# Cross-attention in a decoder layer: the scores of both token halves in one run of matmuls, the value products of both halves in another

## The chip, the cores and the metric

The kernel runs on one core of a Trainium2 chip. The metric is device time in microseconds of one execution, from the first to the last instruction with what lies around them. Names used below: PE is TensorE (matrix products), PEld its weight loads, DVE is VectorE, ACT ScalarE, POOL GpSimd, SP the engine whose queue issues most transfers.

## The reference

One decoder layer over 32 sequences of 64 tokens, width 512, everything in fp32: block-sparse self-attention, cross-attention to a second sequence, and a feed-forward part, each followed by a residual sum and a layer norm. Only the cross-attention is touched here:

```
q = (x @ Wq + bq).reshape(B, L, 8, 4, 128)            # 32 query heads, 8 key heads
k, v = split(ctx @ Wkv + bkv)                          # 8 key heads of 128
scores = einsum('blkgd,bmkd->bkglm', q, k) / sqrt(128) # 64 x 64 for each sequence and head
o = einsum('bkglm,bmkd->blkgd', softmax(scores), v)
x = layernorm(x + o.reshape(B, L, 4096) @ Wo + bo)
```

## The kernel before

The cross-attention stage works on 32 units `n`: eight key heads `g` (outer) by four blocks `tb` of 512 tokens (inner). One block holds eight sequences of 64 tokens; its two halves `pr` = 0 and 1 are 256 tokens each. A unit needs queries for four heads (`qx`), scores (`sx`), a softmax, transposed probabilities (`pTx`), value products (`pox`) and a projection back to width 512 (`wx`).

The query and output projections are each done as seven products of halved matrices instead of eight (a Strassen-like scheme). A product is one `step(i)` of class `Queries` or `Projection`: `mul` (the matmuls at L282) issues 4 matmuls of 128x128 weights with 256 columns, in the trace 8 passes, into one of three banks x, y, z; `read` then lets DVE (or ACT) add the bank into its destination. Two steps that use the same bank follow the same rule in both kernels: the later one waits until the earlier one has been read. For a projection the reads are L345 (one 128x512 sum) and, in step 1, L353 as well (128x1024). The left operands of steps 3, 5, 6 and 7 of a projection are sums that POOL makes from the attention output (`output_sums`, L256 to L259).

`scores(n, pr)` puts 16 small matmuls (128 rows by 64 columns, 64 columns moving, in the trace 32 passes) into a bank, then DVE and ACT do the softmax of this half: row maxima `mxx` (L1048), subtraction `ex` (L1050), exponential on ACT (L1051), sums `denx` (L1053), reciprocal (L1054), product (L1055, both inputs in SBUF), block transposition `Tx` (L1060). `move(n)` issues eight transfers on SP that give `pTx`. `attend(n, pr)` is four matmuls with 64 weight rows, two of them on the lower and two on the upper half of the array (8 passes), into two banks `po0` and `po1`; ACT and DVE empty these with two activations and two additions of the bias each (L1108, L1110).

PE and POOL follow the order written out in the loop over `n`; DVE's and ACT's order comes from the scheduler. While unit `n` makes queries and scores, unit `n-1` is attended and projected. The order on PE for an inner `n`, `q` for query steps and `w` for projection steps:

```
q1 q6 q5 q7 q2  attend(n-1,0)  q4  attend(n-1,1)  q3  w1  scores(n,0)  w6 w5  scores(n,1)  w7 w2 w4 w3
```

In every second unit POOL has four more operations here: for `tb` = 1 the sums of the next token block, for `tb` = 3 those of the next query weights. In the units of the first head (`g` = 0) it adds the output bias to the running sum, four operations of the same size.

PSUM has eight banks in this stage: four shared ones (tag `ps`), two for scores, one each for `po0` and `po1`.

Of the kernel before, what the change touches and what calls it, by code (L numbers as in the profile page):

```python
# [9 lines left out]
F32 = mybir.dt.float32  # L10
I32 = mybir.dt.int32
AF = mybir.ActivationFunctionType
ALU = mybir.AluOpType
# [3 lines left out]
P = 128  # L17
DIM = 512
NH, NKV, HD = 32, 8, 128
REP = NH // NKV  # L20
NT = 2048
SEQ = 64
# [30 lines left out]
def decoder_layer(  # L53
# [30 lines left out]
    nc = tc.nc  # L84
# [91 lines left out]
    HF = DIM // 2  # L176
# [71 lines left out]
    def output_tiles(name):  # L248
        return [big.tile([P, 2, TB], F32, tag=f"oT{j}", name=f"{name}_{j}") for j in range(2)]
# [214 lines left out]
    with ExitStack() as ph:  # L464
# [143 lines left out]
        def scores(n, i):  # L608


            g, tb, h = units[n]
            u = f"{g}_{tb}_{h}_{i}"
            s = sc.tile([P, 2, 512], F32, tag="sc", name=f"s{u}")
            for a in range(2):
                nc.tensor.matmul(  # L615
                    s[:, a, :HALF], qTs[n // REP][:, units[n][2], i * P : (i + 1) * P],
                    kTs[g][:, a * HALF : (a + 1) * HALF], start=True, stop=True,
                )
            nmax = small.tile([P, 1], F32, tag="nmax", name=f"nmax{u}")
            nc.vector.tensor_reduce(nmax, s[:, :, :HALF], AX.XY, ALU.max, negate=True)  # L620
            p = sb.tile([P, NKEY], F32, tag="p", name=f"p{u}", bufs=4)
            den = small.tile([P, 1], F32, tag="den", name=f"den{u}")
            nc.scalar.activation(  # L623
                p.rearrange("q (a k) -> q a k", a=2), s[:, :, :HALF], AF.Exp,
                bias=nmax, accum_out=den,
            )
            if i == 0:
                Ts[n] = sb.tile([P, NBK, TPB, SQ], F32, tag="T", name=f"T{g}_{tb}_{h}")
                flush()
            else:  # L630
                turn(n, i - 1)
            nc.vector.reciprocal(den, den)  # L632
            nc.vector.tensor_scalar(p, p, den, None, ALU.mult)  # L633
            ps_[n, i] = p
            if i == TPB - 1:
                turn(n, i)
# [301 lines left out]
    with ExitStack() as ph:  # L938
# [74 lines left out]

        NPR = TPB // 2
        units = [(g, tb) for g in range(NKV) for tb in range(NTB)]
        kvs, qTs, Ts, pTs, oTs, pjs = {}, {}, {}, {}, {}, {}

        def load_kv(n):
            g, tb = units[n]
# [10 lines left out]
            q = Queries(wq_cur[g], right.pop(n), qTs[n], f"q{u}", XYZ, bias)  # L1030
            return q

        def scores(n, pr):
            g, tb = units[n]
            u = f"x{g}_{tb}_{pr}"
            s = sc.tile([P, 2 * REP, SEQ], F32, tag="sc", name=f"s{u}")
            for i in range(2):
                for h in range(REP):
                    for b in range(2):
                        c0 = (2 * pr + i) * P + b * SEQ  # L1040
                        nc.tensor.matmul(  # L1041
                            s[b * SEQ : (b + 1) * SEQ, i * REP + h, :],
                            qTs[n][:, h, c0 : c0 + SEQ], kvs[n][:, pr, 0, c0 - pr * HF : c0 - pr * HF + SEQ],
                            start=True, stop=True,
                        )
            shape = [P, 2 * REP, SEQ]
            mx = small.tile([P, 2 * REP], F32, tag="mx", name=f"mx{u}")
            nc.vector.tensor_reduce(mx, s, AX.X, ALU.max)  # L1048
            e = sb.tile(shape, F32, tag="e", name=f"e{u}")
            nc.vector.tensor_tensor(e, s, mx[:, :, None].to_broadcast(shape), ALU.subtract)  # L1050
            nc.scalar.activation(e, e, AF.Exp, scale=SCALE)  # L1051
            den = small.tile([P, 2 * REP], F32, tag="xden", name=f"den{u}")
            nc.vector.tensor_reduce(den, e, AX.X, ALU.add)  # L1053
            nc.vector.reciprocal(den, den)  # L1054
            nc.vector.tensor_tensor(e, e, den[:, :, None].to_broadcast(shape), ALU.mult)  # L1055


            if pr == 0:
                Ts[n] = sb.tile([P, 2, TPB * REP, SQ], F32, tag="T", name=f"Tx{g}_{tb}", bufs=1)
            nc.vector.transpose(  # L1060
                Ts[n][:, :, pr * 2 * REP : (pr + 1) * 2 * REP, :].rearrange("p k r j -> p r k j"),
                e.rearrange("p r (k i) -> p r k i", i=SQ),
            )
# [13 lines left out]
                        )  # L1077
            pTs[n] = pT

        def attend(n, pr):  # L1080
            g, tb = units[n]
            if pr == 0:
                oTs[n] = output_tiles(f"oTx{g}_{tb}")
            o5 = [o.rearrange("d h (t b q) -> d t b h q", t=TPB, b=2) for o in oTs[n]]
            po = [
                pp.tile([P, 2, REP * SEQ], F32, tag=f"po{b}", name=f"pox{g}_{tb}_{pr}_{b}")
                for b in range(2)
            ]
            for i in range(2):
                for b in range(2):  # L1090
                    r = slice(b * SEQ, (b + 1) * SEQ)
                    t = 2 * pr + i
                    nc.tensor.matmul(  # L1093
                        po[b][:, i, :].rearrange("d (h a j) -> d h a j", h=REP, a=2),
                        kvs[n][r, pr, 1, i * HD : (i + 1) * HD],
                        pTs[n][r, :, t * P : (t + 1) * P].rearrange("p a (h j) -> p h a j", h=REP),
                        start=True, stop=True,
                    )

            bias = bv[:, g : g + 1]  # L1100
            for b in range(2):
                for j in range(2):
                    dst = o5[j][:, 2 * pr : 2 * pr + 2, b, :, :]
                    src = po[b][:, :, j * HF // 2 : (j + 1) * HF // 2].rearrange(
                        "d i (h q) -> d i h q", h=2
                    )
                    if b == 0:
                        nc.scalar.activation(dst, src, AF.Identity, bias=bias)  # L1108
                    else:
                        nc.vector.tensor_scalar(dst, src, bias, None, ALU.add)  # L1110
            if pr == 1:
                left = output_sums(oTs.pop(n), f"sox{g}_{tb}")
                pjs[n] = Projection(left, wo_cur[g], tb, f"wx{g}_{tb}", XYZ)
                del pTs[n], kvs[n]

        def project(n, *steps):
            g, tb = units[n]
            for i in steps:
                pjs[n].step(i)
                pjs[n].read()  # L1120
            if steps[-1] == 3:
                del pjs[n]
                if g == NKV - 1:
                    layernorm(tb, "x")
                    later.append(lambda: transpose_block(tb, "x2"))
# [84 lines left out]
        for n in range(N + 1):  # L1210
            if n < N:
                g, tb = units[n]
                q = queries(n)
                for i in (1, 6, 5, 7):
                    q.step(i)
                    q.read()
                q.corner()
                q.step(2)


                behind = g > 0 and tb == 1
                if not behind:
                    next_tokens(n + 1, 0)
            if n > 0:
                attend(n - 1, 0)
            while later:
                later.pop(0)()
            if n < N:
                q.step(4)
                q.read()  # L1230
            if n > 0:
                attend(n - 1, 1)
            if n < N:
                q.step(3)
                q.read()
                if behind:
                    next_tokens(n + 1, 0)
                next_tokens(n + 1, 1)
            if n == N:
                feed_forward(1)  # L1240
            if n > 0:
                project(n - 1, 1)
            if n < N:
                if n + 1 < N:
                    load_kv(n + 1)
                scores(n, 0)
            if n < N and g == 0:
                for j in range(TPB):
                    a = acc[tb][:, j, :]
                    nc.gpsimd.tensor_tensor(a, a, bo, ALU.add)  # L1250
            if n > 0:
                project(n - 1, 6, 5)
            if n < N:
                scores(n, 1)
                move(n)
                if tb == NTB - 1 and g + 1 < NKV:
                    load_xq(g + 1)
            if n > 0:
                project(n - 1, 7, 2, 4, 3)
                if n < N and tb == 0:  # L1260
                    if g > 0:
                        load_xo(g)
                    if g == NKV - 1:
                        load_ffn()
            if n == N - 1:
                feed_forward(0)
# [53 lines left out]
```

## Time and profile before

| what | us |
| --- | --- |
| median of 3 runs (3109.12 to 3114.3) | 3110.07 |
| the profiled execution, its own time | 3110.94 |
| its span, first to last instruction | 3109.0 |
| first scores of unit 0, of unit 1, of unit 31 | 2068.86, 2091.02, 2977.11 |
| from one unit's first scores to the next unit's, inner units | 29.26 after even n, 29.45 after odd n |
| PE, DVE, POOL busy over the whole span | 3059.1, 2199.3, 971.6 |

The stage starts at 2068.86 and its last value products are at 3016; the self-attention before it and the feed-forward part after it are the same in both kernels. Since a unit is repeated 32 times, a tenth of a microsecond in a unit is about 3 us in the total.

### The profile page before, as it was taken

The numbers are of one execution on the slowest core, as the hardware profiler recorded it, in microseconds if no ns is written. First come the engines' busy times: TensorE is split into PE (matmuls) and PEld (weight loads), VectorE is DVE, ScalarE is ACT, GpSimd is POOL, SyncE is SP. The second block draws the span as 40 slices with busy tenths as digits, with TensorE's granted clock in tenths as the row PEclk, the third lists the DMA queues.
The fourth block names the chain that finished last, engine by engine and source line by source line (L and its number), as shares of the span: only waits on it lengthen the run. The fifth ranks groups of instructions, "written<-read, shape, count | busy, mean of one in ns | idle before, by whom it ended". The sixth has DMA issues, their size and how long they took to land.

```text
span 3109.0 us, 42300 instructions
## 1 busy us (share of the span) xinstructions
PE 3059.1 (98%) x14944; PEld 2312.8 (74%) x14944; DVE 2199.3 (71%) x3957; ACT 757.3 (24%) x1760; POOL 971.6 (31%) x789
## 2 busy tenths in 40 slices
PE   8999999999999999999999999999999999999998
PEld 5677677777777777677777669988888888888864
DVE  6777777877877877877877754346666666656777
ACT  2323222222232232222322312211111111111222
POOL 3231321321322322223213122135454444444421
PEclk9999999999999999999999999999999999999999
DMA  6444444444454444444444453221121121121101
GB/s 203 118 112 119 113 115 123 111 123 112 107 130 111 107 123 118 105 126 115 114 110 110 100 140 121 101 94 48 53 64 48 51 66 48 48 69 48 48 28 41
DMA packets 200913, 298.66 MB, mean 96 GB/s; under 512 B 44160, under 2 KB 94848, under 8 KB 200704
## 3 DMA queue, kind: packets, MB, share of 16 engines
q1 hardware_dynamic: 187328, 282.51, 33.7%
q10 hardware_dynamic: 11328, 9.26, 1.0%
q0 software_dynamic: 2048, 4.20, 0.5%
q8 instruction: 120, 1.97, 0.3%
q14 instruction: 89, 0.73, 0.1%
HBM read 107.05 MB, written 20.97 MB: 41 GB/s over the span
## 4 chain that ended last, share of the span: by engine, by line
PE 91%; DVE 4%; DMA 2%; SPq 2%; ACT 1%; issue 1%; ACTq 0%; DVEq 0%
PE po L661 15%; PE s L615 15%; PE sx L1041 2%; PE pox L1093 2%; PE wx_0y L282 1%; PE wx_2y L282 1%; PE wx_1y L282 1%; SPq L653 1%; PE w_0y L282 1%; PE q_3y L282 1%; PE w_3y L282 1%; PE qx_0y L282 1%; PE qx_3y L282 1%; PE wx_3y L282 1%; PE q_2y L282 1%; PE w_1y L282 1%
## 5 line engine op out<-in xcount | busy, mean ns | idle before, releaser
L623 ACT ACTIVATE p<-s,nmax 128x576 f32<-128x576 f32 x512 | 379.2, 741 | 1213.6 <-DVE nmax L620 1210.6
L615 PE MATMUL s<-kT,qT 128*128 128x288 f32 x2048 | 578.0, 408 | 11.6 <-ACT p L623 10.8
L661 PE MATMUL po<-pT,v 128*128 128x512 f32 (+1 forms) x1280 | 549.3, 602 | 4.6 <-DMA pT<-T 4.6
L615 PEld LDWEIGHTS s<-kT,qT 128*128 128x128 f32 x2048 | 387.5, 190 | 116.5 <-issue 20.1
L620 DVE TENSOR_REDUCE nmax<-s 128x1 f32<-128x576 f32 x512 | 383.8, 750 | 48.9 <-PE s L615 48.3
L641 DVE STREAM_TRANSPOSE T<-p 128x576 f32<-128x576 f32 x512 | 393.8, 769 | 4.4
L661 PEld LDWEIGHTS po<-pT,v 128*128 128x128 f32 (+1 forms) x1280 | 213.6, 189 | 205.0 <-issue 177.6
L633 DVE TENSOR_SCALAR p<-p,den 128x576 f32<-128x576 f32 x512 | 324.9, 635 | 17.9
L632 DVE RECIPROCAL den<-den 128x1 f32<-128x1 f32 x512 | 83.9, 164 | 238.3 <-ACT p L623 238.3
L256 POOL TENSOR_TENSOR so<-oT,oT 128x512 f32<-128x512 f32 x32 | 42.6, 1330 | 651.1 <-ACT oT L684 651.1
L258 POOL TENSOR_TENSOR so<-oT 128x512 f32<-128x512 f32 x32 | 40.7, 1272 | 334.0 <-PE w_1y L282 93.0
L1051 ACT ACTIVATE ex<-ex 128x512 f32<-128x512 f32 x64 | 40.4, 631 | 328.1 <-DVE ex L1050 328.1
L1197 POOL TENSOR_TENSOR txx<-x1T 128x512 f32<-128x512 f32 x31 | 39.4, 1269 | 237.1 <-PE qx_3z L282 95.7
L197 POOL TENSOR_TENSOR tx<-xT 128x512 f32<-128x512 f32 x31 | 39.7, 1280 | 206.9 <-PE q_3z L282 65.5
L623 ACT ACTIVATION_READ_ACCUMULATOR p<-s,nmax 128x1 f32 x512 | 99.0, 193 | 0.0
L1110 DVE TENSOR_SCALAR oTx<-pox,bv 128x256 f32<-128x256 f32 x128 | 56.1, 478 | 47.8 <-PE pox L1093 47.8
L256 POOL TENSOR_TENSOR sox<-oTx,oTx 128x512 f32<-128x512 f32 x32 | 40.5, 1266 | 151.2 <-DVE oTx L1110 146.2
L684 ACT COPY oT<-po 128x512 f32<-128x512 f32 x128 | 71.8, 586 | 45.0 <-PE po L661 44.1
L1041 PEld LDWEIGHTS sx<-kvx,qTx 128*64 128x64 f32 x2048 | 64.8, 138 | 20.9 <-issue 11.3
L1093 PE MATMUL pox<-pTx,kvx 64*128 64x256 f32 x512 | 73.3, 402 | 1.4 <-DMA pTx<-Tx 1.4
L1041 PE MATMUL sx<-kvx,qTx 128*64 128x64 f32 x2048 | 73.5, 225 | 0.0
L1108 ACT ACTIVATE oTx<-pox,bv 128x256 f32<-128x256 f32 x128 | 53.7, 470 | 79.0 <-PE pox L1093 79.0
(445 smaller groups left out, 5786.5 us busy)
## 6 DMA issues: line engine op xcount, KB each, us to landing
pT<-T SPq DMA_DIRECT2D x1020, 80.0 KB, 2.1
pT<-T SPq DMA_DIRECT2D x1016, 64.0 KB, 2.0
xT<-in_xT SPq DMA_DIRECT2D x31, 1024.0 KB, 5.7
kvx<-kv SPq DMA_DIRECT2D x32, 512.0 KB, 3.3
pTx<-Tx SPq DMA_DIRECT2D x256, 64.0 KB, 2.0
kv<-c SPq DMA_DIRECT2D x30, 512.0 KB, 2.6
wo<-in_woT SPq DMA_DIRECT2D x32, 256.0 KB, 3.0
xwq<-in_xwq SPq DMA_DIRECT2D x32, 256.0 KB, 2.8
```

Of the source, the lines that this page charges most:

```text
L256: nc.gpsimd.tensor_tensor(t[1], a[1, 0], a[1, 1], ALU.add)
L282: nc.tensor.matmul(self.banks[b][:, m, :], self.left[i][:, k, m * P : (m + 1) * P], self.right[i][:, k, :], start=(first and m + k == 0), ...
L615: nc.tensor.matmul(s[:, a, :HALF], qTs[n // REP][:, units[n][2], i * P : (i + 1) * P], kTs[g][:, a * HALF : (a + 1) * HALF], start=True, s ...
L620: nc.vector.tensor_reduce(nmax, s[:, :, :HALF], AX.XY, ALU.max, negate=True)
L623: nc.scalar.activation(p.rearrange("q (a k) -> q a k", a=2), s[:, :, :HALF], AF.Exp, bias=nmax, accum_out=den,)
L632: nc.vector.reciprocal(den, den)
L633: nc.vector.tensor_scalar(p, p, den, None, ALU.mult)
L641: nc.vector.transpose(Ts[n][:, :, i, :], ps_.pop((n, i)).rearrange("q (b k) -> q b k", k=SQ))
L661: nc.tensor.matmul(pos[n].rearrange("d (a q) -> d a q", a=NQD), vs[units[n][0]][rows, v, :], pTs[n // 2][rows, :, chunk, :], skip_group_ch ...
L684: nc.scalar.copy(o[:, i, :].rearrange("d (t a k) -> d a t k", t=TPB, a=NQD), pos.pop(n - 1 + i).rearrange("d (a t k) -> d a t k", a=NQD, t ...
L1041: nc.tensor.matmul(s[b * SEQ : (b + 1) * SEQ, i * REP + h, :], qTs[n][:, h, c0 : c0 + SEQ], kvs[n][:, pr, 0, c0 - pr * HF : c0 - pr * HF + ...
L1093: nc.tensor.matmul(po[b][:, i, :].rearrange("d (h a j) -> d h a j", h=REP, a=2), kvs[n][r, pr, 1, i * HD : (i + 1) * HD], pTs[n][r, :, t * ...
```

## The change

`scores(n)` now issues the 32 small matmuls of both halves together and keeps both banks; the softmax of each half is a function of its own. `attend(n)` issues the value products of both halves together: the first half still goes to `po0` and `po1`, the second half to two of the four shared banks, and the emptying follows in the order half, head pair, batch. The loop places the joined `attend` behind query step 4, and the projection steps after the scores come as 6, 5, 2, 7, 3, 4:

```
q1 q6 q5 q7 q2  q4  attend(n-1)  q3  w1  scores(n)  w6 w5  w2 w7 w3 w4
```

```diff
-        def scores(n, pr):
+        def scores(n):
+            for pr in range(2):
+                g, tb = units[n]
+                s = sc.tile([P, 2 * REP, SEQ], F32, tag="sc", name=f"sx{g}_{tb}_{pr}")
+                for i in range(2):
+                    for h in range(REP):
+                        for b in range(2):
+                            c0 = i * P + b * SEQ
+                            nc.tensor.matmul(
+                                s[b * SEQ : (b + 1) * SEQ, i * REP + h, :],
+                                qTs[n][:, h, pr * HF + c0 : pr * HF + c0 + SEQ],
+                                kvs[n][:, pr, 0, c0 : c0 + SEQ], start=True, stop=True,
+                            )
+                ss[n, pr] = s
+
+        def softmax(n, pr):
             g, tb = units[n]
             u = f"x{g}_{tb}_{pr}"
-            s = sc.tile([P, 2 * REP, SEQ], F32, tag="sc", name=f"s{u}")
...
+            s = ss.pop((n, pr))
             shape = [P, 2 * REP, SEQ]
             mx = small.tile([P, 2 * REP], F32, tag="mx", name=f"mx{u}")
             nc.vector.tensor_reduce(mx, s, AX.X, ALU.max)
...
-        def attend(n, pr):
+        def attend(n):
...
-            po = [
-                pp.tile([P, 2, REP * SEQ], F32, tag=f"po{b}", name=f"pox{g}_{tb}_{pr}_{b}")
-                for b in range(2)
-            ]
+            po = {}
+            for pr in range(2):
                 for b in range(2):
+                    name = f"pox{g}_{tb}_{pr}_{b}"
+                    po[pr, b] = (bank([P, 2, REP * SEQ], name) if pr else
+                                 pp.tile([P, 2, REP * SEQ], F32, tag=f"po{b}", name=name))
+                for i in range(2):
+                    for b in range(2):
...
+                        nc.tensor.matmul(
+                            po[pr, b][:, i, :].rearrange("d (h a j) -> d h a j", h=REP, a=2),
...
-            for b in range(2):
+            for pr in range(2):
                 for j in range(2):
+                    for b in range(2):
...
@@ project
-            if steps[-1] == 3:
+            if steps[-1] == 4:
@@ loop over n
-            if n > 0:
-                attend(n - 1, 0)
             while later:
                 later.pop(0)()
             if n < N:
                 q.step(4)
                 q.read()
             if n > 0:
-                attend(n - 1, 1)
+                attend(n - 1)
...
-                scores(n, 0)
+                scores(n)
+                softmax(n, 0)
...
                 project(n - 1, 6, 5)
             if n < N:
-                scores(n, 1)
+                softmax(n, 1)
                 move(n)
...
-                project(n - 1, 7, 2, 4, 3)
+                project(n - 1, 2, 7, 3, 4)
```

The scheduler's order on DVE behind the joined scores, for an inner unit (0 and 1 are the halves, `w6` is the read of projection step 6, and so on):

```
w1 (L345, L353)  max0 max1  sub0 sub1  w6  sum0 sum1  recip0  w5  prod0  recip1  transp0  prod1  w2  transp1  w7  w3  w4
```

Before, it was:

```
w1 (L345, L353)  max0 sub0  w6  sum0  w5  recip0 prod0  max1  transp0  sub1  w7  sum1  w2  recip1 prod1 transp1  w4  w3
```

More of the change, by code (lines that the diff above doesn't have):

```diff
@@ L1015, in decoder_layer @@
         units = [(g, tb) for g in range(NKV) for tb in range(NTB)]
-        kvs, qTs, Ts, pTs, oTs, pjs = {}, {}, {}, {}, {}, {}
+        kvs, qTs, ss, Ts, pTs, oTs, pjs = {}, {}, {}, {}, {}, {}, {}
         def load_kv(n):
@@ L1031, in queries @@
             return q
-        def scores(n, pr):
+        def scores(n):
[13 more added lines that the diff above has]
+        def softmax(n, pr):
             g, tb = units[n]
             u = f"x{g}_{tb}_{pr}"
-            s = sc.tile([P, 2 * REP, SEQ], F32, tag="sc", name=f"s{u}")
-            for i in range(2):
-                for h in range(REP):
-                    for b in range(2):
[L1040 to L1045, printed above, removed]
+            s = ss.pop((n, pr))
             shape = [P, 2 * REP, SEQ]
@@ L1078, in move @@
             pTs[n] = pT
-        def attend(n, pr):
+        def attend(n):
             g, tb = units[n]
-            if pr == 0:
-                oTs[n] = output_tiles(f"oTx{g}_{tb}")
+            oTs[n] = output_tiles(f"oTx{g}_{tb}")
             o5 = [o.rearrange("d h (t b q) -> d t b h q", t=TPB, b=2) for o in oTs[n]]
-            po = [
-                pp.tile([P, 2, REP * SEQ], F32, tag=f"po{b}", name=f"pox{g}_{tb}_{pr}_{b}")
-                for b in range(2)
-            ]
-            for i in range(2):
-                for b in range(2):
[L1091 to L1098, printed above, removed]
+            po = {}
+            for pr in range(2):
+                for b in range(2):
+                    name = f"pox{g}_{tb}_{pr}_{b}"
[3 more added lines that the diff above has]
+                    for b in range(2):
+                        r = slice(b * SEQ, (b + 1) * SEQ)
+                        t = 2 * pr + i
+                        nc.tensor.matmul(
+                            po[pr, b][:, i, :].rearrange("d (h a j) -> d h a j", h=REP, a=2),
+                            kvs[n][r, pr, 1, i * HD : (i + 1) * HD],
+                            pTs[n][r, :, t * P : (t + 1) * P].rearrange(
+                                "p a (h j) -> p h a j", h=REP
+                            ),
+                            start=True, stop=True,
+                        )
@@ L1100, in attend @@
             bias = bv[:, g : g + 1]
-            for b in range(2):
+            for pr in range(2):
                 for j in range(2):
[L1103 to L1114, printed above, removed]
+                    for b in range(2):
+                        dst = o5[j][:, 2 * pr : 2 * pr + 2, b, :, :]
+                        src = po[pr, b][:, :, j * HF // 2 : (j + 1) * HF // 2].rearrange(
+                            "d i (h q) -> d i h q", h=2
+                        )
+                        if b == 0:
+                            nc.scalar.activation(dst, src, AF.Identity, bias=bias)
+                        else:
+                            nc.vector.tensor_scalar(dst, src, bias, None, ALU.add)
@@ L1116, in project @@
+            left = output_sums(oTs.pop(n), f"sox{g}_{tb}")
+            pjs[n] = Projection(left, wo_cur[g], tb, f"wx{g}_{tb}", XYZ)
+            del pTs[n], kvs[n]
         def project(n, *steps):
```

## The prediction

> **What bounds the kernel now.** The page first: busy shares and the chain that ended last.
>
> ```profile
> PE 3059.1 (98%) x14944; PEld 2312.8 (74%) x14944; DVE 2199.3 (71%) x3957; ACT 757.3 (24%) x1760; POOL 971.6 (31%) x789
> PE 91%; DVE 4%; DMA 2%; SPq 2%; ACT 1%; issue 1%; ACTq 0%; DVEq 0%
> ```
>
> PE is the bound, and in the cross-attention stage it has no idle time that the list of waits would show: between 2060 and 3020 us PE waits 5.8 us in all. So a gain must come from inside PE's stream. Next the timeline of PE in an inner unit, n = 10 (start, length, steps in order; a length reaches to the end of the last pass, so I read distances between starts):
>
> ```profile
> 2358.01 1.89 PE L282 MATMUL wx_1z<-xwo,sox 128*128 128x256 f32 x8
> 2359.84 1.15 PE L1041 MATMUL sx<-kvx,qTx 128*64 128x64 f32 x32
> 2360.92 1.99 PE L282 MATMUL wx_1y<-xwo,sox 128*128 128x256 f32 x8
> 2362.75 1.89 PE L282 MATMUL wx_1x<-xwo,oTx 128*128 128x256 f32 x8
> 2364.47 1.89 PE L282 MATMUL wx_1y<-xwo,oTx 128*128 128x256 f32 x8
> ...
> 2376.65 1.14 PE L1093 MATMUL pox<-pTx,kvx 64*128 64x256 f32 x8
> 2377.72 1.99 PE L282 MATMUL qx_3y<-txx,xwq 128*128 128x256 f32 x8
> 2379.64 1.13 PE L1093 MATMUL pox<-pTx,kvx 64*128 64x256 f32 x8
> 2380.71 1.99 PE L282 MATMUL qx_3z<-x1T,xwq 128*128 128x256 f32 x8
> ```
>
> A product between two others takes 1.73 (2362.75 to 2364.47). A product before a run of small matmuls takes 1.83 (2358.01 to 2359.84), and so does the one behind it (2360.92 to 2362.75): each change of the array's shape costs PE 0.10 on both sides, beside what is lost inside the run. A joined run of scores is in this trace already, in unit 0, which has no projection to put between:
>
> ```profile
> 2068.87 2.09 PE L1041 MATMUL sx<-kvx,qTx 128*64 128x64 f32 x64
> 2070.88 1.99 PE L282 MATMUL qx_1x<-x1T,xwq 128*128 128x256 f32 x8
> ```
>
> 64 passes in 2.01, against 2 x 1.08 for two runs of 32.
>
> Last, who else is close behind PE. Timeline of all engines in an odd unit, n = 9 (the lines that matter):
>
> ```profile
> 2330.79 1.27 POOL L1199 TENSOR_TENSOR txx<-x1T 128x512 f32<-128x512 f32 x1
> 2331.33 1.28 DVE L1055 TENSOR_TENSOR ex<-ex,denx 128x512 f32<-128x512 f32 x1
> 2332.02 1.72 POOL L1194 TENSOR_TENSOR txx<-x1T,txx 128x512 f32<-128x512 f32 x1
> ...
> 2333.30 1.89 PE L282 MATMUL wx_0x<-xwo,oTx 128*128 128x256 f32 x8
> ...
> 2334.33 0.67 DVE L345 TENSOR_TENSOR acc<-wx_0y,acc 128x512 f32<-128x512 f32 x1
> ...
> 2335.14 1.97 PE L282 MATMUL wx_0y<-xwo,oTx 128*128 128x256 f32 x8
> ```
>
> The softmax product L1055 takes 1.28 here and 0.69 in the even unit: it stands still until POOL's L1199 is over (2332.06) and ends 0.55 later; POOL's next operation is stretched in turn and ends 1.13 after the product. DVE is then so late that its read of w7 ends at 2335.00, and w4, which writes the same bank, starts 0.14 later. It was due at 2335.03; with 0.08 more on its first passes the odd unit loses 0.19. That is the difference of the two periods, 29.45 and 29.26. So DVE has no slack at this very place: read of w7, then w4 in the same bank.
>
> **The change part by part.** Let S be the first score matmul of a unit.
>
> *Joined scores.* Saved: 2 x 1.08 - 2.01 = 0.15, and one pair of changes of shape, 0.195. Together 0.345 a unit, 31 units.
>
> *Joined value products.* Their pairs of passes follow at 0.22, the first at 0.32 (starts 2376.65, 2376.97, 2377.19). Four more pairs in a running group cost 0.86, so the joined run takes 1.07 + 0.86 = 1.93 against 2.13: 0.20, and 0.195 for the changes of shape, 0.40 a unit. The least it can be is 0.195, if the change of bank in the middle costs as much as a new run; the nearest row, the joined scores, changes banks in its middle too and loses nothing, so I take 0.40. The second half needs two shared banks. Their former users are a read on ACT after q2, over by 0.9 while q4 alone takes 1.73, and a projection step of the unit before: no wait. Sum so far: 0.745 a unit.
>
> Here the Trainium skill says, in "TensorEngine Tiling (Array Packing)", Tiling Modes, that a change of the tiling mode drains the array, while tiles of one mode run on independently. It gives no time; the rows give 0.345 and 0.40. By that rule alone the change is worth 31 x 0.745 = 23 us.
>
> *q4 ahead of the value products.* q4 needs the read of q7: behind n = 10 it runs from 2375.04 to 2375.73 (L325), and q2 ends at 2376.65. The sum txx4 on POOL is a unit old. No cost. Transfers of pTx get 1.8 more time; they start earlier as well, since the transpositions end at S + 10.2 instead of S + 11.8. Only unit 0 waited for them (1.42 in the list of waits, 1.80 beyond the normal spacing): about 1.7 saved, once. SP's queue keeps its order.
>
> *Emptying pox and output sums.* ACT needs 4 x 0.42, DVE 4 x 0.43 behind two query reads of 0.43. The first half is emptied while the second half runs, so the last eviction ends about 1.0 after the run, as before; POOL's sums start 2.5 before S, as before. w6 now starts 2.0 behind S instead of 1.1, so that dependency gets looser.
>
> *DVE behind the scores.* This is where the gain goes. Both softmaxes now start at once, and the read of w7 has moved behind both. Spacings from n = 10 in the timeline: 0.61 for a 512-wide operation, 0.72 if the next one needs its result, 1.13 for L353, 0.19 for a reciprocal, 0.63 for a transposition. From S: w1 0.11 (as in n = 10), L353 0.72, max0 1.85, max1 2.45, sub0 3.06, sub1 3.67, w6 4.28, sum0 4.89 (exponential 0 over at 4.4), sum1 5.50, recip0 6.11, w5 6.30, prod0 6.91, recip1 7.52, transp0 7.71, prod1 8.34, w2 8.95, transp1 9.56, w7 10.19 to 10.85. DVE never waits for PE in this chain. PE comes to w4 at 2.01 + 1.83 + 4 x 1.73 = 10.75; by the pattern of unit 9 it starts 0.14 behind DVE, at 10.99, and loses 0.08 more: a stall of 0.30 where before there was none. Even unit: -0.745 + 0.30 = **-0.445**.
>
> *Odd units.* POOL's operations stand, from S, as in the trace of before: for tb = 1 the last one runs from 6.37 to 7.64, so prod0 (6.91) ends at 8.19 instead of 7.60, +0.59; stall 0.89, of which 0.19 was there: -0.745 + 0.89 - 0.19 = **-0.045**. For tb = 3 L192 runs to 7.75, prod0 +0.70; L193 then ends 1.13 behind it, at 9.43, and holds prod1 too, +0.25: stall 1.25, net **+0.315**. In g = 0 POOL's four bias sums run from S + 3.8 to S + 9.2 over both products; I put the stall between those two, 1.08, less 0.07 of before: **+0.27** for n = 1, 2, 3.
>
> Here a rule speaks against the change: "SBUF — State Buffer", Who interferes with whom, has it that a DVE operation with two SBUF inputs and a POOL operation that reads SBUF exclude each other for the whole instruction. The rows of n = 9 agree (1.28 and 1.72 for 0.69 and 1.27). If the products were not held up, all 17 odd and early units would come out like the even ones: instead of 7 x -0.045 + 7 x 0.315 + 3 x 0.27 = +2.7 they would give 17 x -0.445 = -7.6, and the sum below would be -14.8 (3095). I follow rule and row.
>
> *Sum.* Unit 0 to 1: -0.40 for its value products, -1.7 for the transfers, -2.1. Even units 4 to 30: 14 x -0.445 = -6.2. The others +2.7. In the last head DVE also has the layer norms of two blocks in its queue just as w7's read is due, and the value products of the last unit lose the transposes between them as a cover: +1.1, an estimate (0 to +2.5). Total **-4.5 us**: 3110.94 - 4.5 = 3106.4 for an execution like the profiled one, which was 0.87 above the median; against the median, 3105.6.
>
> **The rivals.**
>
> *PE keeps the gain.* If w7's read comes in time everywhere, 31 x 0.745 + 1.7, and the 2.9 that odd and early units lose today, 27.7 us: 3082. For it: PE is 98% busy and DVE 71%. Against it: DVE is at its limit just here, as unit 9 shows. Halfway lies a DVE chain shorter by 0.3 (a 0.02 shorter spacing in 15 operations does it): then even units keep 0.745, the others gain 0.3 as well, 9.3 more, -13.8 us: 3096.
>
> *Slower: POOL's hold on the products decides.* If prod0 and prod1 are both held in all units (POOL's sums later by 3 us than I lay them out reach S + 6.9 in even units too), every unit pays what tb = 3 pays: 28 x 0.315 + 0.8 - 2.1 + 1.1 = +8.6, 3118.7. It decides from the point where w7's read ends 0.45 later than 10.85 in an even unit. For it: POOL is busy a third of the span and each clash costs up to a whole POOL operation. Against it: in even units POOL is done with txx4 at S + 3.8.
>
> *It does not do what it says.* If the joined value products break at the change of bank, 0.20 a unit is lost: 6 us, 3111.8.
>
> **How the numbers follow.** Forecast 0.64; PE keeps more of its gain 0.22 (0.13 halfway, 0.09 in full); slower or no join 0.14. An error of 0.1 in the stall of a unit is 3 us, so the forecast's own range is 3100 to 3111. The range over the cases is 3096 to 3115: it reaches to the halfway case and takes in the broken join, and leaves out the full gain (0.09) and most of the slower case (0.07). A change under 0.2%, 6.2 us, is about what a measurement of this kernel cannot tell from none. Faster by more: 0.20 from the forecast, 0.21 from the first rival, 0.41. Slower by more: 0.03 and 0.10, 0.13. Within: 0.46.
>
> **What would show it.** In the trace after: sx in runs of 64 with 2.0 to the next product, pox in runs of 16 with 1.93; w4 (the last wx y of a unit) starting late by 0.3 in even and about 1 in odd units, 0.14 behind the L345 of w7; products of 1.28 in odd units, two of them for tb = 3; periods of 28.8, 29.4 and 29.75. Wrong would be: periods of 28.5 without a gap ahead of w4 (DVE has slack), runs of pox still in eights, or a gap at another step.

## The result and the profile after

| | before | after |
| --- | --- | --- |
| median of 7 runs each, us | 3110.07 (3105.87 to 3114.3) | 3098.92 (3097.46 to 3099.89) |
| ratio after / before, 95% | | 0.9962 [0.9953, 0.9971] |
| profiled execution, its own time; its span | 3110.94; 3109.0 | 3099.28; 3097.0 |
| unit 0 to unit 1, first scores to first scores | 22.16 | 20.03 |
| n = 1, 2, 3 (first head) | 29.32 each | 29.42, 29.48, 29.47 |
| even units | 29.25 | 28.51 |
| tb = 1; tb = 3 | 29.45; 29.45 | 29.22; 29.70 |
| n = 29; n = 30 | 32.79; 31.63 | 32.26; 32.42 |
| first scores of unit 31 to the end | 131.87 | 132.76 |

The kernel is faster by 11.15 us, 0.38%; the forecast was 4.5 us faster. The 3098.92 lies 1 us below the range of that forecast (3100 to 3111) and inside the range over all cases (3096 to 3115). Run again beside other kernels, the same changed kernel had a median of 3099.24 and a ratio of 0.9972 [0.9960, 0.9983], with periods of 28.51, 29.22 and 29.70 in its trace:

> The changed kernel once more, beside the version above on one chip, for a comparison of the two and for how much the part ahead of the cross-attention differs between executions: periods 28.51, 29.22 and 29.70 again, 3099; first scores of unit 0 anywhere between 2065 and 2069.

From the profiles, the stage from the first scores of unit 0 to those of unit 31 went from 908.24 to 897.26, and 0.9 came back behind it: 10.1 us (9.4 in the repeat). The span shrank by 12.0, because the stage also began 1.8 earlier, at 2067.03; with the same code ahead of it the stage began anywhere from 2065.5 to 2068.9 in the twelve traces of this case, and at 2068.7 in the repeat, so these 1.8 are not the change's. All that follows is about periods inside the stage. As in the prediction, S is the start of a unit's first score matmul, w4 is the step that writes the bank which DVE's read of w7 empties, and odd units are those with tb = 1 or tb = 3.

The page after, busy shares and the chain that ended last:

```profile
PE 3038.2 (98%) x14944; PEld 2318.1 (75%) x14944; DVE 2184.0 (71%) x3957; ACT 754.8 (24%) x1760; POOL 967.6 (31%) x789
PE 86%; DVE 10%; DMA 1%; SPq 1%; issue 1%; ACT 1%; DVEq 0%; ACTq 0%
```

PE is as full as before, but DVE's part of the chain rose from 4% to 10%: wherever PE waits for a read, the chain now runs back through DVE's work behind the scores. The list of PE's waits between 2060 and 3020 us (total, times, longest) names them and shows in which token blocks they fall; its first three lines:

```profile
PE wx_2y L282 <- DVE acc L345: 6.8, 8, 0.9
PE wx_0y L282 <- DVE acc L345: 3.8, 8, 0.6
PE wx_1y L282 <- DVE acc L345: 1.3, 2, 0.7
```

`wx_0` and `wx_2` are the projections of blocks 0 and 2, done in units tb = 1 and tb = 3. They wait eight times each, once a head. `wx_1` belongs to even units and waits twice in all (n = 2 and n = 30, in the first and the last head), and `wx_3`, the other even ones, is not in the list.

PE in an even unit, n = 10, and the first line of n = 11 (start, length, step):

```profile
2349.11 2.08 PE L1043 MATMUL sx<-kvx,qTx 128*64 128x64 f32 x64
2351.12 1.99 PE L282 MATMUL wx_1y<-xwo,sox 128*128 128x256 f32 x8
...
2358.14 1.89 PE L282 MATMUL wx_1z<-xwo,sox 128*128 128x256 f32 x8
2359.86 1.89 PE L282 MATMUL wx_1y<-xwo,oTx 128*128 128x256 f32 x8
...
2372.04 2.00 PE L1103 MATMUL pox<-pTx,kvx 64*128 64x256 f32 x16
2373.97 1.99 PE L282 MATMUL qx_3z<-x1T,xwq 128*128 128x256 f32 x8
...
2377.62 2.08 PE L1043 MATMUL sx<-kvx,qTx 128*64 128x64 f32 x64
```

64 score passes take 2.01 (2349.11 to 2351.12) and 16 value passes 1.93 (2372.04 to 2373.97), both as forecast. The `wx_1y` of 2359.86 is w4. It starts 1.72 behind its predecessor, the plain distance of two products, so there is no gap ahead of it, though the forecast had 0.30 there. The timeline of all engines from the same S = 2349.11 shows DVE's side:

```profile
2355.13 0.19 DVE L1062 RECIPROCAL denx<-denx 128x8 f32<-128x8 f32 x1
2355.24 0.64 DVE L345 TENSOR_TENSOR acc<-wx_1z,acc 128x512 f32<-128x512 f32 x1
2355.80 0.68 DVE L1063 TENSOR_TENSOR ex<-ex,denx 128x512 f32<-128x512 f32 x1
...
2356.39 0.19 DVE L1062 RECIPROCAL denx<-denx 128x8 f32<-128x8 f32 x1
...
2356.51 0.71 DVE L1068 STREAM_TRANSPOSE Tx<-ex 128x512 f32<-128x512 f32 x1
...
2358.94 0.65 DVE L345 TENSOR_TENSOR acc<-wx_1y,acc 128x512 f32<-128x512 f32 x1
```

The last line is the read of w7, from S + 9.83 to S + 10.48; the forecast had S + 10.19 to S + 10.85. Behind each reciprocal the next operation starts 0.11 or 0.12 later (2355.13 to 2355.24, 2356.39 to 2356.51), not 0.19.

Odd units look as the forecast drew them. Timeline of n = 9, a tb = 1 unit with S = 2319.89:

```profile
2326.25 1.28 POOL L1206 TENSOR_TENSOR txx<-x1T,txx 128x512 f32<-128x512 f32 x1
2326.58 1.50 DVE L1063 TENSOR_TENSOR ex<-ex,denx 128x512 f32<-128x512 f32 x1
...
2330.54 0.65 DVE L345 TENSOR_TENSOR acc<-wx_0y,acc 128x512 f32<-128x512 f32 x1
...
2331.25 1.99 PE L282 MATMUL wx_0y<-xwo,oTx 128*128 128x256 f32 x8 [0.44 <-DVE acc L345]
```

The product stands until POOL's last sum is over (2327.53) and ends 0.55 later. Then the read of w7 ends at 2331.19, S + 11.30, and w4 follows 0.06 behind it, instead of at S + 10.75. The tb = 3 unit n = 11, S = 2377.62:

```profile
2384.11 1.26 POOL L192 TENSOR_TENSOR xwq<-xwq,xwq 128x512 f32<-128x512 f32 x1
2384.31 1.61 DVE L1063 TENSOR_TENSOR ex<-ex,denx 128x512 f32<-128x512 f32 x1
...
2385.45 1.60 POOL L193 TENSOR_TENSOR xwq<-xwq,xwq 128x512 f32<-128x512 f32 x1
...
2386.60 1.01 DVE L1063 TENSOR_TENSOR ex<-ex,denx 128x512 f32<-128x512 f32 x1
...
2388.75 0.65 DVE L345 TENSOR_TENSOR acc<-wx_2y,acc 128x512 f32<-128x512 f32 x1
...
2389.45 1.78 PE L282 MATMUL wx_2y<-xwo,oTx 128*128 128x256 f32 x7 [0.92 <-DVE acc L345]
```

Both products are held, by L192 and by L193. The read of w7 ends at S + 11.78 and w4 is 1.08 late.

### The profile page after: what moved, and what is told of

Read it like the earlier page. It is cut to its first block, busy times and chain, and to the rows that moved or that the text cites. A ratio compares the mean times of both kernels' runs of the same rounds, so it can differ in the third digit from the quotient of the medians.

```text
span 3097.0 us, 42303 instructions
## 1 busy us (share of the span) xinstructions
PE 3038.2 (98%) x14944; PEld 2318.1 (75%) x14944; DVE 2184.0 (71%) x3957; ACT 754.8 (24%) x1760; POOL 967.6 (31%) x789
## 4 chain that ended last, share of the span: by engine, by line
PE 86%; DVE 10%; DMA 1%; SPq 1%; issue 1%; ACT 1%; DVEq 0%; ACTq 0%
PE po L661 15%; PE s L615 15%; PE pox L1103 2%; DVE acc L345 2%; SPq L653 1%; PE w_0y L282 1%; PE q_3y L282 1%; PE w_3y L282 1%; PE qx_3y L282 1%; PE qx_2y L282 1%; PE qx_0y L282 1%; PE q_2y L282 1%; PE w_1y L282 1%; PE qx_1y L282 1%; PE wx_3y L282 1%; PE q_0y L282 1%
## 5 line engine op out<-in xcount | busy, mean ns | idle before, releaser
L1043 PE MATMUL sx<-kvx,qTx 128*64 128x64 f32 x2048 | 66.7, 224 | 0.0
L1103 PE MATMUL pox<-pTx,kvx 64*128 64x256 f32 x512 | 64.5, 389 | 0.1
```

Of the source, the lines that this page charges most:

```text
L1043: nc.tensor.matmul(s[b * SEQ : (b + 1) * SEQ, i * REP + h, :], qTs[n][:, h, pr * HF + c0 : pr * HF + c0 + SEQ], kvs[n][:, pr, 0, c0 : c0 + ...
L1103: nc.tensor.matmul(po[pr, b][:, i, :].rearrange("d (h a j) -> d h a j", h=REP, a=2), kvs[n][r, pr, 1, i * HD : (i + 1) * HD], pTs[n][r, :, ...
```

## The experiments

The theory: the two joins save PE 0.345 and 0.40 in every unit, and what is given back depends on one thing, when DVE has finished its read of w7 compared with w4, which writes the same bank. How late that read is follows from the order of DVE's operations and, in odd units, from POOL holding up the softmax products. The rivals: the joins save less than counted and something else in the new order makes up for it; or the odd units are long for another reason than POOL. All ratios are against the kernel before on the same chip.

**Each join alone.** The kernel before with the scores joined and the softmax as a function of its own; value products in two runs and projection order 7, 2, 4, 3 as before:

```diff
-                scores(n, 0)
+                scores(n)
+                softmax(n, 0)
...
-                scores(n, 1)
+                softmax(n, 1)
```

> The kernel before with the scores joined and nothing else; the projection order behind them stays w6 w5 w7 w2 w4 w3. Theory (PE saves 0.345 a unit by the join; w4 may start only 0.14 after DVE has read w7 from the same bank, and both softmaxes now stand ahead of that read): w7 is read about 0.6 earlier than in the changed kernel, but PE comes to w4 1.7 earlier, so w4 waits about 0.5 in even units and 1.3 to 1.7 in odd ones. Periods 29.4 (even), 30.2 (tb = 1), 30.6 (tb = 3); total about 18 us slower than before, 3128. Rival (only changes of shape count, DVE has room): even periods 28.9, about 11 us faster than before.

Measured: 3131.35, ratio 1.0074 [1.0058, 1.0091]; periods 29.39, 30.21 and 30.68. PE's waits in the stage:

```profile
PE wx_2y L282 <- DVE acc L345: 12.3, 8, 1.8
PE wx_0y L282 <- DVE acc L345: 8.8, 8, 1.3
PE wx_1y L282 <- DVE acc L345: 4.6, 8, 1.8
PE wx_3y L282 <- DVE acc L345: 1.8, 7, 0.3
```

The saving is there, but more than the saving is lost again: every kind of unit waits. In this order w4 is due one product earlier, at S + 2.01 + 1.83 + 3 x 1.73 = S + 9.03, and the timeline of n = 10 (S = 2358.70) has

```profile
2367.30 0.68 DVE L345 TENSOR_TENSOR acc<-wx_1y,acc 128x512 f32<-128x512 f32 x1
...
2368.13 1.96 PE L282 MATMUL wx_1y<-xwo,oTx 128*128 128x256 f32 x8 [0.25 <-DVE acc L345]
```

w4 starts at S + 9.43, 0.40 late, and the step behind it starts 1.80 after w4 instead of 1.73: 29.25 - 0.345 + 0.40 + 0.07 = 29.38, against 29.39 measured.

The kernel before with the value products joined behind q4 and nothing else (the loop; `attend` is the joined one of the change):

```diff
-            if n > 0:
-                attend(n - 1, 0)
             while later:
...
-                attend(n - 1, 1)
+                attend(n - 1)
```

> The kernel before with the value products joined behind q4 and nothing else. Theory: DVE's order behind the scores is that of before, so nothing is given back there: 0.40 saved in every unit, periods 28.86 (even) and about 29.0 (odd), 1.7 saved once at unit 0; about 13 us faster than before. Rival (joined value products break at the change of bank and give only the change of shape): 0.2 a unit, periods 29.06, about 8 us faster.

Measured: 3093.60, ratio 0.9947 [0.9930, 0.9963]; periods 28.86 (even) and 28.99 (odd). That is 0.39 off the even units and 0.46 off the odd ones, and 12.6 us over the 31 units. The odd ones gain the difference at w4, which starts 0.05 behind the read of w7 here and 0.15 behind it in the kernel before; why is open. PE's timeline at the value products:

```profile
2371.20 2.00 PE L1095 MATMUL pox<-pTx,kvx 64*128 64x256 f32 x16
2373.12 1.99 PE L282 MATMUL qx_3z<-x1T,xwq 128*128 128x256 f32 x8
```

1.92 for 16 passes: the change of bank in the middle costs nothing that can be seen. One join of the two, by itself, gains as much as the whole change did or more (12.6 in the stage against 11.0; 1.5 and 0.9 of it came back behind the stage, and the intervals of the two ratios overlap); the other, by itself, loses 19.7 (S0 to S31 927.97).

**The projection order.** The changed kernel with the old order 7, 2, 4, 3 (the condition on the last step goes with it):

```diff
-                project(n - 1, 2, 7, 3, 4)
+                project(n - 1, 7, 2, 4, 3)
```

> The changed kernel with the projection steps behind the scores in the order of before, w7 w2 w4 w3 instead of w2 w7 w3 w4. Theory (w4 starts 0.14 after DVE's read of w7): DVE reads w7 where it read w2 before, about 1.2 earlier, but PE comes to w4 1.73 earlier, so even units stall by about 0.5, tb = 1 by 1.3, tb = 3 by 1.7: periods 29.0, 29.8, 30.2 instead of 28.51, 29.22, 29.70; about 16 us slower than the changed kernel, 3115. Rival (the order of the projection steps is of no account once the runs are joined): 28.51 and 3099.

Measured: 3116.47, ratio 1.0026 [1.0016, 1.0037]; periods 28.93, 29.75, 30.23. This order costs 0.4 to 0.5 in every kind of unit. So the new order is not a tidying beside the joins: it moves w4 one product away from w7, and without it the whole change makes the kernel slower.

**POOL's hold on the products.** The changed kernel with the exponential written back to the scores' bank in PSUM, so that the sum and the product read one operand there instead of two in SBUF; the amount of work is the same:

```diff
-            nc.scalar.activation(e, e, AF.Exp, scale=SCALE)
+            nc.scalar.activation(s, e, AF.Exp, scale=SCALE)
...
-            nc.vector.tensor_reduce(den, e, AX.X, ALU.add)
+            nc.vector.tensor_reduce(den, s, AX.X, ALU.add)
...
-            nc.vector.tensor_tensor(e, e, den[:, :, None].to_broadcast(shape), ALU.mult)
+            nc.vector.tensor_tensor(e, s, den[:, :, None].to_broadcast(shape), ALU.mult)
```

> The changed kernel, with the exponential written back into the score bank in PSUM, so that the row sums and the softmax product read one large operand from PSUM and only one input from SBUF. POOL's work and its order are as they were. Theory (POOL's hold on a product with two SBUF inputs makes the odd units slow): no product of 1.28 any more, odd and even units alike; the scheduler also puts the second row sum one place later on DVE, which costs up to 0.3 in all units: periods 28.5 to 28.8 in all of them instead of 28.51, 29.22 and 29.70; about 3 to 10 us faster than the changed kernel. Rival (odd units are slow because PE waits for POOL's sums themselves): odd periods stay at 29.2 and 29.7.

Measured: 3092.28, ratio 0.9943 [0.9926, 0.9960]; all inner periods 28.75, even and odd, but for one of 28.91. The product's group on DVE between 2070 and 2960 us (busy, mean ns), first of the changed kernel, then of this one:

```profile
L1063 DVE TENSOR_TENSOR ex<-ex,denx 128x512 f32<-128x512 f32 x62 | 57.6, 932 | 0.0
```

```profile
L1063 DVE TENSOR_TENSOR ex<-sx,denx 128x512 f32<-128x512 f32 x62 | 41.2, 667 | 0.0
```

With one operand in PSUM the product takes 667 ns on average beside the same POOL operations, and the difference of odd and even units is gone. In n = 9 it starts at 2326.67 and takes 0.68 while POOL's L1206, begun at 2325.98, takes its usual 1.27. That settles that POOL's hold makes the odd units longer. The even units lose 0.24 here for another reason: the scheduler has put the read of w5 ahead of the second sum, and DVE stands idle for 0.26 until PE has finished w5 (n = 10, 2353.89 to 2354.15). The read of w7 then ends at S + 10.84.

The same edit in the kernel before:

> The kernel before with nothing joined; only the exponential is written back into the score bank, so that the softmax product has one SBUF input. Theory (POOL's hold is what makes odd units longer in the kernel before, by 0.19): all periods 29.25, products of about 0.69 everywhere, 2.9 us faster than before. Rival (odd units are longer for POOL's sums): 29.25 and 29.45 stay, no difference.

Measured: 3107.29, ratio 0.9997 [0.9988, 1.0005]. Its trace has periods of 29.25 in all inner units, as expected, and the read of w7 ends at S + 8.76 in odd units as in even ones (S + 9.34 in the odd units of the kernel before), so the old 0.19 between odd and even units was POOL's hold as well. The 2.1 us that this took off the stage (908.24 to 906.09) are too few for the comparison of times to tell.

**The place of the value products.** The changed kernel with the joined `attend` ahead of q4, where the first half stood:

```diff
+            if n > 0:
+                attend(n - 1)
             while later:
...
-            if n > 0:
-                attend(n - 1)
```

> The changed kernel with the joined value products ahead of q4 instead of behind it; DVE's order behind the scores is the same. POOL's sums of the attention output then start 1.7 earlier before the scores, so POOL's extra operations are over earlier too. Theory (hold on the products): for tb = 1 POOL is done before the first product, period 28.51 to 28.6; for tb = 3 only the last operation still meets it, about 28.9; even units stay at 28.51. Unit 0 waits for its transfers again, +1.7. In all about 9 us faster than the changed kernel, 3090. Rival (place of the value products does not matter): 28.51, 29.22 and 29.70 as in the changed kernel, and 1.7 us slower for the transfers.

Measured: 3095.90, ratio 0.9958 [0.9944, 0.9972]; periods 28.64 (even and tb = 1) and 29.05 (tb = 3). PE's timeline:

```profile
2367.91 2.13 PE L1103 MATMUL pox<-pTx,kvx 64*128 64x256 f32 x16
2369.96 1.99 PE L282 MATMUL qx_3y<-txx,xwq 128*128 128x256 f32 x8
```

2.05 instead of 1.93. One of the two banks of the second half is the one that ACT's two reads of q2 leave (L317, 2368.01 to 2368.85 in the same timeline), and without q4 in between PE reaches it at about the time they end. The list of waits has no line for it, but the single passes show it: those into the other bank keep their times (2368.87, 2369.09), and those into this one start at 2368.90, 0.05 behind ACT's last read, and then 0.32 apart instead of 0.22. The 0.12 are gone in the last version below, where q2 comes one step earlier. The expected 28.51 missed them, and the stage became 6.2 shorter than the changed kernel's where about 9 had been expected. In return POOL's sums start one product earlier. They are clear of the products when tb = 1, where the period falls by 0.58, and still hold one of them when tb = 3.

Taking this further, the last version keeps `attend` ahead of q4, puts q2 ahead of q7 so that its bank is free in time, and moves the fourth sum of the next query weights (L193 of the changed kernel) on POOL behind the next unit's token sums:

```diff
-                for i in (1, 6, 5, 7):
+                for i in (1, 6, 5):
                     q.step(i)
                     q.read()
-                q.corner()
                 q.step(2)
+                q.step(7)
+                q.read()
+                q.corner()
...
+                while late_sum:
+                    late_sum.pop(0)()
+            if n > 0:
+                attend(n - 1)
```

> A version that should beat both: the changed kernel with the joined value products ahead of q4, query steps 1 6 5 2 7 (so that ACT has read q2 before the value products want its bank), and the fourth sum of the next query weights on POOL moved behind the token sums of the next unit. Theory: POOL is done before the first softmax product in all units with g > 0, the value products run in 1.93, even and odd units all at 28.51; about 29.3 to 29.6 stays in two or three units of g = 0, where POOL adds the bias. From unit 1 to unit 31 about 10 us less than the changed kernel: 3088. Rival (even units have no slack of their own, so the earlier value products push DVE): even units above 28.6, gain under 6 us.

Measured: 3091.20 (3088.66 to 3096.33), ratio 0.9953 [0.9939, 0.9966]; all periods between the first and the last head are 28.51, and the value run is back at 1.93. Its first unit is 3.2 longer than in the changed kernel (23.24), mainly since the value products wait for their transfers there again (2.9 in the list of waits). Of all versions this one has the shortest stage, 887.33. The timeline of n = 11 (S = 2378.44), where POOL and the first product stood in each other's way:

```profile
2383.55 1.27 POOL L192 TENSOR_TENSOR xwq<-xwq,xwq 128x512 f32<-128x512 f32 x1
...
2385.13 0.69 DVE L1069 TENSOR_TENSOR ex<-ex,denx 128x512 f32<-128x512 f32 x1
...
2389.20 1.89 PE L288 MATMUL wx_2y<-xwo,oTx 128*128 128x256 f32 x8
```

POOL is done 0.31 ahead of the product (0.69, as in an even unit), and w4 starts at S + 10.76. PE keeps the 0.745 in every one of these units. Its ratio cannot be told from those of the exponential in PSUM, of the value join alone or of the two reciprocals below.

**The order on DVE or the amount of its work.** If the time of w7's read is all that counts, more work for DVE must cost exactly what it delays that read, and nothing if it doesn't. Two reciprocals a unit are added whose result is not used:

```diff
             nc.vector.reciprocal(den, den)
+            if pr == 0:
+                for z in range(2):
+                    nc.vector.reciprocal(mx, den)
```

With these the scheduler puts the read of w7 ahead of the second transposition instead of behind it, and the read of w2 ahead of the second product.

> The changed kernel with two more tiny reciprocals on DVE in the softmax of half 0 (result unused). The scheduler answers by putting the read of w7 ahead of the second transposition, so DVE has more to do but comes to w7 earlier. Theory (only the moment at which w7 has been read counts, not DVE's work): w7 is read about 0.4 earlier than in the changed kernel, even units stay at 28.51, tb = 1 falls to about 28.75 and tb = 3 to 28.8 (one product less is held); about 9 us faster than the changed kernel, 3090. Rival (DVE's total work behind the scores counts): two operations more of 0.11, all periods longer by up to 0.2, slower.

Measured: 3090.01, ratio 0.9930 [0.9914, 0.9947]; periods 28.51, 28.70, 28.82. More work on DVE, and a faster kernel: its ratio and that of the changed kernel are apart, and it beats both kernels. DVE in n = 10 (S = 2350.02):

```profile
2359.36 0.69 DVE L345 TENSOR_TENSOR acc<-wx_1y,acc 128x512 f32<-128x512 f32 x1
2359.96 0.70 DVE L1071 STREAM_TRANSPOSE Tx<-ex 128x512 f32<-128x512 f32 x1
```

The read of w7 starts at S + 9.34, 0.49 earlier than in the changed kernel, and the transposition stands behind it. The counterpart has four such reciprocals, with which the order of the large operations is again the changed kernel's:

> The changed kernel with four more tiny reciprocals on DVE in the softmax of half 0 (result unused); here the order of the large operations stays that of the changed kernel. Theory (in even units of the changed kernel the read of w7 ends at S + 10.48, 0.13 too early to hold w4): four times 0.11 ahead of it put its end at S + 10.9, w4 waits 0.3 and loses 0.08 more, even units at 28.9 to 29.0, odd ones longer by up to 0.4 too, about 10 us slower than the changed kernel. Rival (even units have slack of 0.5 or more): 28.51 in even units.

Measured: 3104.77, ratio 0.9984 [0.9977, 0.9991]; periods 28.77, 29.53, 29.70. In n = 10 (S = 2349.42):

```profile
2359.00 0.70 DVE L1071 STREAM_TRANSPOSE Tx<-ex 128x512 f32<-128x512 f32 x1
2359.63 0.66 DVE L345 TENSOR_TENSOR acc<-wx_1y,acc 128x512 f32<-128x512 f32 x1
```

The read ends at S + 10.87, and the even unit is 0.26 longer, a little less than the 0.4 to 0.5 expected: four more operations delayed the read by 0.39, and the first 0.13 of it were slack. The stage is 6.3 us longer than in the changed kernel (903.60), where about 10 had been expected. Units of tb = 3 did not change, since there the delay falls into the time for which POOL holds the product anyway.

**One rule for all of these.** In the kernels with the projection order 2, 7, 3, 4 and joins as in the changed kernel:

| kernel and unit | w7's read ends, behind S | period measured | 28.51 + (end - 10.61), not under 28.51 |
| --- | --- | --- | --- |
| two more operations, even | 10.03 | 28.51 | 28.51 |
| changed kernel, even | 10.48 | 28.51 | 28.51 |
| exponential in PSUM, tb = 3 | 10.84 | 28.75 | 28.74 |
| four more operations, even | 10.87 | 28.77 | 28.77 |
| two more operations, tb = 3 | 10.90 | 28.82 | 28.80 |
| changed kernel, tb = 1 | 11.30 | 29.22 | 29.20 |
| changed kernel, tb = 3 | 11.78 | 29.70 | 29.68 |

10.61 is w4's due time, 10.75, less 0.14. In the traces the loss behind a late read has two parts: w4 starts 0.06 behind the end of the read, and the step behind it then starts 1.83 after w4 instead of 1.73. They make 0.16, hence the last 0.02 of the table. Seven kinds of unit from four kernels lie within 0.02 of one line, and the tb = 1 units of the kernels with two and with four more operations, not listed, lie there too (28.70 and 29.53). Nothing else needs to be assumed for the inner units of these kernels.

## Why the prediction was right in direction and too small

Its steps, against the trace after:

- *Joined scores -0.345, joined value products -0.40*: right. The even period is 29.25 - 0.745 = 28.51 to the hundredth; the value run alone gave 0.39. That the value run might break at the change of bank is ruled out.
- *Unit 0 to 1, -2.1*: measured -2.13, which is partly luck. In the repeat it was -1.25, since the value products there still waited 0.6 for their transfers, where the forecast had them wait for nothing.
- *Even unit, a stall of 0.30 ahead of w4*: **this is the step that failed.** The stall is zero. The chain behind S has the order that the prediction gave, but the read of w7 ended at S + 10.48 instead of S + 10.85. Of the 0.37, 0.16 are the two reciprocals (a spacing of 0.11 or 0.12 taken as 0.19, which is the length of the operation in its row), and the rest is a sum of small ones: spacings of 0.56 to 0.60 where 0.61 was taken, 0.09 up to the first reciprocal and about 0.12 behind it. The spacings came from the kernel before, where each reciprocal is followed at once by the operation that needs it. There the distance is 0.23, so the old rows do not give the new spacing. In the new order something independent stands behind it. In 13 even units, 0.30 too much made 3.9 us. (The parts of that stall, 10.99 - 10.75 and 0.08, add up to 0.32; it was entered as 0.30.)
- *tb = 1, -0.045*: measured -0.23. The product's end at S + 8.19 was right, but the operations behind it were closer together, and the read ended at S + 11.30 where the sum had 11.44. The loss behind the read was 0.16 as well, where 0.14 and 0.08 had been read off the kernel before. Six units, 1.1 us.
- *tb = 3, +0.315*: measured +0.25. L192's end at S + 7.75 and L193's at S + 9.43 were met, and both products were held as described; the read ended at S + 11.78 where the sum had 11.80, and most of the 0.06 is the smaller loss at w4.
- *First head, +0.27 each*: measured +0.41 in sum for the three where +0.81 was forecast. Their stall was 0.91 to 0.97 where 1.08 had been put between two other cases.
- *Last head, +1.1*: n = 29 to the end came to +1.15 where the sum had -0.045 - 0.445 + 0.315 + 1.1 = +0.9. The 0.315 is for n = 31, counted as a seventh unit of tb = 3; POOL has no next query weights to sum there, so that nothing holds its products, and the nearness of the two figures is no test of the +1.1, which was an estimate.

Together 10.1 us saved in the stage instead of 4.5. The mechanism was right; the term to blame is the length of one chain of eighteen DVE operations (the prediction speaks of 15), wrong by 0.37 of 10.85, because the result depends on it by a threshold: an even unit had 0.24 of stall by the arithmetic of the bank, and had 0.13 to spare in fact. The prediction saw this in its halfway rival ("a 0.02 shorter spacing in 15 operations does it"), which puts the gain at 13.8; what happened is that case, except that units held by POOL gained less than 0.3 from the shorter chain, because the hold absorbs what arrives early. That case had 0.13 of the chance.

The slower rival, a hold in all units, was not what happened, and its mechanism is real: it is what makes odd units cost more than even ones. The rule of the Trainium skill, "SBUF — State Buffer", Who interferes with whom, was followed and is borne out here: products of 1.50 and 1.61 where 0.68 was due, and 667 ns on average once one operand is in PSUM.

What stays open: why the two parts of the loss at w4 behind a late read are about 0.15 and 0.07 in some kernels and 0.06 and 0.10 in others; why the time at which the stage begins varies by up to 3.4 us between executions with the same code ahead of it (by up to 2.1 on one chip), and the division of the 1.15 us of the last head among layer norms and value products, which was not taken apart.

## What to carry to other kernels

Joining small matmuls of one shape was worth here what the rows of the kernel before say, per run removed, but the engine that empties the banks then gets its work in one lump. Look for the next matmul that writes a bank of that lump and compare its due time with the end of the read: below the threshold a delay costs nothing, above it it costs its full length in every iteration. When such a chain decides, take the spacing of each pair from operations in the same relation (needing the result or not), and treat a result within a few per cent of the threshold as two cases of nearly equal chance. The order of DVE's operations and the place of their operands can be worth more than their number: two useless operations that moved two reads forward, one operand left in PSUM, or POOL's sums started a product earlier each took about 6 us more off the stage (897.26 to 891.06, 890.99 and 891.10).

## What the runs showed of the hardware that had not been expected

- Behind a reciprocal of 128x8 DVE started an operation that doesn't need its result after 0.11 us; where the next one needed it, as in the kernel before, the distance was 0.23. The kind of operation is not the reason: the softmax product, at 0.23 behind its own reciprocal in the kernel before (2360.55 to 2360.78), starts 0.11 behind an added one whose result it does not use (2356.70 to 2356.81 in the kernel with two more).
- A product that finds POOL in its last operation loses only what is left of that operation: in the changed kernel it ends 0.55 or 0.56 behind POOL in all three cases shown above. In the kernel with two more reciprocals, tb = 3, where more stands ahead of it on DVE, the second product began after POOL's last sum and took 0.68, where it takes 1.01 in the changed kernel.
